# Graph attention layer: the last 20 nodes' four head pairs in one step instead of four

## The chip, the core and the metric

The kernel runs on one core of a Trainium2 chip. TensorE multiplies matrices (its array has 128 rows and 128 columns and can be split into parts that hold different weights), VectorE, ScalarE (ACT) and GpSimd (POOL) work on elements, and SyncE (SP) issues most of the DMA transfers. Each engine works through its own instructions in order and waits on semaphores for the others. The metric is the device time of one execution in microseconds; the time of the kernel before is the median of three runs.

## The reference

Four graph layers follow one another on 2708 nodes with 512 features, each with a residual and a layer norm. The change touches layer 0 alone, an attention over the neighbours with 8 heads of 64 features:

```python
adj = jnp.maximum(adjacency_matrix, jnp.eye(n))
keys    = jnp.einsum('nj,hjk->hnk', node_matrix, Wks)
queries = jnp.einsum('nj,hjk->hnk', node_matrix, Wqs)
values  = jnp.einsum('nj,hjk->hnk', node_matrix, Wvs)
atts = jnp.einsum('hqk,hmk->hqm', queries, keys) / key_dim ** 0.5
atts = atts - 1e+16 * (1.0 - adj)[None, :, :]
atts = jax.nn.softmax(atts, axis=-1)
return jnp.einsum('hqm,hmk,hko->qo', atts, values, Wo)
...
x = _layernorm(x + _L0_gnn_ref(x, adj, ...), axis=-1)
```

Every node's query meets the keys of all 2708 nodes, in every head; the mask lets only neighbours count.

## The kernel before, in words

**Projections.** Keys, values and queries of all nodes are computed first. Keys stay in the on-chip memory as `KT` (features on partitions, two heads of 64 on the two halves of 128), values as `V`, queries go out to memory (`qtd`).

**Items.** The nodes are cut into 22 chunks of 128 rows; the last has 2708 - 21*128 = 20. An item (line 447) is one chunk `c` and one of four head pairs `p`, so there are 88. The class `Pair` (line 276) holds an item's steps. The 2708 keys are taken in three batches of 1024, 1024 and 660, each in two parts of at most 512[...].

- `scores` (line 293): for each part, two products on TensorE, one for each head `j` on its half of the array's rows (line 308), then two reductions on VectorE (line 316) that add the mask, write the scores and keep the row maximum. In the last chunk only 20 partitions are used; there POOL first clears the scores' tile.
- `maxima` (331), then `weights` (338): ACT takes the exponential and the row sums, which go to `smt`.
- `blocks` (353) and `deal` (363): for the first two batches, VectorE transposes blocks of 32x32, and SP moves them by DMA so that keys lie on partitions. `turn` (369): the third batch is transposed by TensorE (382, 389, 391) and copied by ACT (383, 392, 393).
- `values` (398): the weights times `V`, 22 chunks of keys for two heads, summed up on TensorE (410); ACT copies the sum (420) and POOL stores it (421). There is one such accumulator, so a new item's first sum waits for the old item's copy.

**Order.** The loop at line 452 writes out the order for TensorE, VectorE and ACT by hand. In iteration `i` four items are in flight: `new` (item `i`) has its scores made, `cur` (item `i-1`) its exponentials, transposes and deals, `late` (item `i-2`) the third and first batch's values, `old` (item `i-3`) the second batch's values and its copy. After the last item three iterations follow that have no new scores. SP and POOL are ordered by the scheduler. The next chunk's adjacency rows and queries are loaded (`load_chunk`, 153) and prepared (row sums 167, diagonal 176, mask 184) while a chunk's four items run.

**Heads' sums.** `heads_sums` and `heads_rows` (425, 438) turn the inverse row sums of half of the chunks into rows in memory (`rs_d`), in the middle and after the last item.

**What follows layer 0's loop.** For each chunk (line 588) SP loads the stored sums (591), the residual (592) and the broadcast inverse row sums (596); POOL multiplies (599), TensorE maps with `Wo` (602), VectorE adds the residual and applies the layer norm. Layers 1 to 3 come after that and are the same in both kernels.

Of the kernel before, what the change touches and what calls it, by code (L numbers as in the profile page):

```python
# [8 lines left out]
F32 = mybir.dt.float32  # L9
# [13 lines left out]
def kernel(  # L23
# [103 lines left out]
    for t in smt:  # L127
        nc.vector.memset(t, 1.0)
    rs_d = [
        dram.tile([c1 - c0, 2, NP, P], F32, tag=f"rs_d{c0}", name=f"rs_d{c0}") for c0, c1 in ((0, HALF0), (HALF0, NC))  # L130
    ]
    otd = [dram.tile([P, NP, rows(c)[1]], F32, tag=f"otd{c}", name=f"otd{c}") for c in range(NC)]
    with ExitStack() as l0:
# [19 lines left out]
        def load_chunk(c, k):  # L153

            r0, q = rows(c)
            if k == 0:
                a = adjp.tile([P, N], F32, tag="adj", name=f"adj{c}")
                qt = io.tile([P, NP, P], F32, tag="qt", name=f"qt{c}")
                loaded[c] = (a, qt)
            a, qt = loaded[c]  # L160
            if k < NW:
                n0, w = batch(k)
                nc.sync.dma_start(a[:q, n0 : n0 + w], adj[r0 : r0 + q, n0 : n0 + w])
            else:
                nc.sync.dma_start(qt[:, :, :q], qtd[c])

# [9 lines left out]
        def loops(c, k):  # L176

            r0, q = rows(c)
            a = loaded[c][0]
            n0, w = batch(k)  # L180
            if n0 <= r0 < n0 + w:
                nc.vector.tensor_tensor(a[:q, r0 : r0 + q], a[:q, r0 : r0 + q], ident[:q, :q], ALU.max)

        def mask(c, k):

            q = rows(c)[1]
            n0, w = batch(k)
            a = loaded[c][0][:q, n0 : n0 + w]
            nc.scalar.activation(a, a, AF.Identity, scale=1e16, bias=far[:q])
# [86 lines left out]
        class Pair:  # L276


            def __init__(self, c, p):
                self.c, self.p = c, p  # L280
                self.q = rows(c)[1]
                self.groups = (self.q + 31) // 32
# [9 lines left out]

            def scores(self, k, part):

                c, p, q = self.c, self.p, self.q
                a, qt = loaded[c]
                n0, w = batch(k)
                if part == 0:
                    s = sp.tile([P, 2, SW], F32, tag="s", name=f"s{c}_{p}_{k}")
                    if q < P:  # L300
                        nc.gpsimd.memset(s[: 32 * self.groups, :, :w], 0.0)
                    self.s.append(s)
# [4 lines left out]
                for j in range(2):  # L307
                    nc.tensor.matmul(  # L308
                        pss[j][:q, :hw],
                        qt[j * KD : (j + 1) * KD, p, :q],  # L310
                        KT[j * KD : (j + 1) * KD, p, n0 + h0 : n0 + h0 + hw],
                        start=True,
                        stop=True,
                    )
                for j in range(2):
                    nc.vector.tensor_tensor_reduce(  # L316
                        out=s[:q, j, h0 : h0 + hw],
                        in0=pss[j][:q, :hw],
                        in1=a[:q, n0 + h0 : n0 + h0 + hw],
# [4 lines left out]
                        accum_out=self.mx[j][:q, 2 * k + part : 2 * k + part + 1],  # L324
                    )

            def maxima(self):
                c, p, q = self.c, self.p, self.q
                self.nm = [small.tile([P, 1], F32, tag=f"nm{j}", name=f"nm{c}_{p}_{j}") for j in range(2)]
                for j in range(2):  # L330
                    nc.vector.tensor_reduce(self.nm[j][:q], self.mx[j][:q], AX.X, ALU.max, negate=True)  # L331

            def weights(self, k):

                c, p, q, nm = self.c, self.p, self.q, self.nm
                w = batch(k)[1]
                for j in range(2):
                    nc.scalar.activation(  # L338
                        self.s[k][:q, j, :w],
                        self.s[k][:q, j, :w],  # L340
                        AF.Exp,
                        bias=nm[j][:q],
                        accum_out=smt[c // HALF0][:q, c % HALF0, 2 * p + j, k : k + 1],
                    )

            def blocks(self, k, j):

                if k not in self.D:
                    n = ends[k + 1] - ends[k]
                    self.D[k] = dp.tile([P, KD4, 2, n, 32], F32, tag="d", name=f"d{self.c}_{self.p}_{k}")  # L350
                b = 32 * self.groups
                n = ends[k + 1] - ends[k]
                nc.vector.transpose(  # L353
                    self.D[k][:b, :, j].rearrange("p i m x -> p m i x"),
                    self.s[k][:b, j, : n * P].rearrange("p (m i x) -> p m i x", i=KD4, x=32),
                )

            def deal(self, k):
# [3 lines left out]
                for g in range(self.groups):  # L362
# [6 lines left out]
            def turn(self):  # L369

                c, p, q = self.c, self.p, self.q
# [3 lines left out]
                def part(j, m):  # L375
                    return self.s[2][:q, j, (m - ND) * P : (m - ND) * P + P]

                for j in range(2):
                    pt = ps_t.tile([P, last - ND, P], F32, tag="t", name=f"pst{c}_{p}_{j}")
                    sb = ptp.tile([P, last - ND, P], F32, tag="pt", name=f"pt{c}_{p}_{j}", bufs=2)  # L380
                    for m in range(ND, last):
                        nc.tensor.transpose(pt[:, m - ND, :q], part(j, m), ident[:q, :q])  # L382
                    nc.scalar.copy(sb[:, :, :q], pt[:, :, :q])  # L383
                    for m in range(ND, last):
                        self.pts[m, j] = sb[:, m - ND, :q]
                pt = ps_t.tile([P, 4, P], F32, tag="t", name=f"pst{c}_{p}_2")
                sb = ptp.tile([P, 2, P], F32, tag="pt2", name=f"pt{c}_{p}_2")
                for j in range(2):
                    nc.tensor.transpose(pt[:, j, :q], part(j, last), ident[:q, :q])
                for j in range(2):  # L390
                    nc.tensor.transpose(pt[:mr, 2 + j, :q], self.s[2][:q, j, o : o + mr], ident[:q, :q])
                nc.scalar.copy(sb[:, :, :q], pt[:, :2, :q])
                nc.scalar.copy(lastT[:mr, :, :q], pt[:mr, 2:, :q])
                for j in range(2):
                    self.pts[last, j] = sb[:, j, :q]
                    self.pts[NC - 1, j] = lastT[:, j, :q]

            def values(self, m0, m1):
                c, p, q = self.c, self.p, self.q
                if self.av is None:  # L400
                    self.av = ps_a.tile([P, P], F32, tag="av", name=f"av{c}_{p}")
                for m in range(m0, m1):
                    for j in range(2):
                        h = 2 * p + j
                        if m < ND:
                            f = max(f for f in self.E if f <= m)
                            x = self.E[f][:, :, j, m - f, :] if q == P else self.E[f][:, 0, j, m - f, :q]
                        else:
                            x = self.pts[m, j]
                        nc.tensor.matmul(  # L410
                            self.av[j * KD : (j + 1) * KD, :q],
                            V[:, m, h * KD : (h + 1) * KD],
                            x,
                            start=(self.done == 0),
                            stop=(self.done == NC - 1),
                        )
                    self.done += 1
                if self.done == NC:
                    ot = io.tile([P, P], F32, tag="ot", name=f"ot{c}_{p}")
                    nc.scalar.copy(ot[:, :q], self.av[:, :q])  # L420
                    nc.gpsimd.dma_start(otd[c][:, p, :], ot[:, :q])  # L421
# [3 lines left out]
        def heads_sums(i):  # L425

            c0, c1 = (0, HALF0) if i == 0 else (HALF0, NC)
            rs = small.tile([P, NC - HALF0, 2 * NP], F32, tag="rs", name=f"rs{i}", bufs=1)[:, : c1 - c0, :]
            nc.vector.tensor_reduce(
                rs.rearrange("p c h -> p (c h)"), smt[i].rearrange("p c h k -> p (c h) k"), AX.X, ALU.add  # L430
# [16 lines left out]
        items = [(c, p) for c in range(NC) for p in range(NP)]  # L447
        old = late = cur = None
        with tc.manual_schedule(
            engines={mybir.EngineType.PE, mybir.EngineType.DVE, mybir.EngineType.Activation}  # L450
        ):
            for i in range(len(items) + 3):
                new = None
                prep = i < len(items) and items[i][0] + 1 < NC and items[i][1] > 0
                if cur is not None:
                    cur.weights(0)
                if i < len(items):
# [3 lines left out]
                    new = Pair(c, p)  # L461
# [31 lines left out]
                if i in (HALF0 * NP + 2, len(items) + 1):  # L493
                    sums = heads_sums(i > HALF0 * NP + 2)
                if cur is not None:
                    cur.turn()
                if i in (HALF0 * NP + 3, len(items) + 1):
                    heads_rows(*sums)
                old, late, cur = late, cur, new
# [28 lines left out]

    LR = rows(NC - 1)[1]
# [704 lines left out]
```

## Time and profile before

The page is of one profiled execution. Busy time is the share of the span in which an engine had an instruction in work; TensorE's ends are modelled, so its busy time says little about how fast it works. Times in the rows are counted from the start of the span.

| | before |
|---|---|
| time, median of 3 runs | 2624.93 us (2623.91 to 2626.01) |
| the profiled execution: its own time / its span | 2626.93 us / 2625.1 us |
| mean granted clock of TensorE | 0.987 of full speed |
| busy: TensorE, VectorE, ACT, POOL | 2558.7, 1907.4, 1231.2, 332.4 us |
| scores' products, line 308 | 2112 instructions, 484.4 us busy |
| scores' reductions, line 316 | 1056 instructions, 594.4 us busy |
| block transposes, line 353 | 352 instructions, 416.4 us busy |
| first store of a weighted sum / last | 267.5 us / 1283.1 us |
| first product of the last chunk's scores | 1219.15 us |
| first product of the stage after the loop | 1287.38 us |

In a row of the instructions in order of time stand the start, the time that it and its like took together, the engine, the line and operation, the tile written and those read, the part of the array used (rows*columns) with the moving data's shape, and how many instructions are merged. In brackets stands the idle time before it and what ended that. A row of a stretch gives each engine's busy time in it with the number of instructions, the clock granted to TensorE (1.00 is full), the share of time in which the DMA engines were busy, and what they moved.

### The profile page before, as it was taken

How to read it: one execution, taken by the hardware profiler on the slowest of the kernel's cores; microseconds unless marked ns; L12 is line 12 of the kernel's file. 1: busy time of each engine (PE TensorE's matmuls, PEld its weight loads, DVE VectorE, ACT ScalarE, POOL GpSimd, SP SyncE). 2: the span in 40 equal slices, each digit the busy share in tenths (PEclk: the TensorE clock that was granted, in tenths of full speed). 3: DMA queues.
4: the chain of work that ended last, by engine and by line, in shares of the span. 5: the costliest groups of instructions: out<-in, count | busy, mean ns of one | idle time of the engine just before them, and what ended most of it. 6: DMA issues, size and time to landing. Idle time of an engine off the chain costs nothing. (4 is left out here: it accounts for less than half of the span.)

```text
span 2625.1 us, 42264 instructions
## 1 busy us (share of the span) xinstructions
PE 2558.7 (97%) x15298; PEld 1476.8 (56%) x15298; DVE 1907.4 (73%) x4661; ACT 1231.2 (47%) x2464; POOL 332.4 (13%) x336
## 2 busy tenths in 40 slices
PE   8999999999999999999899999899999999999997
PEld 3445677666767676666447444444444456444465
DVE  2004999999999999999684678978767775453544
ACT  1113878788787887877311001566655540000000
POOL 1110000000000000002220000234333330000000
PEclk9999999999999999999799999999999999999999
DMA  5012888888888888887572444354434213644533
GB/s 198 32 53 64 216 233 209 235 211 216 228 214 221 220 208 235 213 212 169 153 240 62 130 122 141 107 166 144 118 101 135 61 30 108 181 142 144 175 100 105
DMA packets 220040, 410.46 MB, mean 156 GB/s; under 512 B 27456, under 2 KB 47664, under 8 KB 219832
## 3 DMA queue, kind: packets, MB, share of 16 engines
q1 hardware_dynamic: 213528, 391.03, 55.4%
q0 software_dynamic: 6304, 16.74, 1.8%
q8 instruction: 121, 1.98, 0.3%
q14 instruction: 87, 0.71, 0.1%
HBM read 212.57 MB, written 16.73 MB: 87 GB/s over the span
## 5 line engine op out<-in xcount | busy, mean ns | idle before, releaser
L316 DVE CUSTOM_DVE_ANT_0 s<-pss,adj 128x512 f32<-128x512 f32 (+3 forms) x1056 | 594.4, 617 | 29.8 <-PE pss L308 27.9
L338 ACT ACTIVATE s<-s,nm 128x1024 f32<-128x1024 f32 (+1 forms) x528 | 546.3, 1037 | 22.2 <-DVE nm L331 20.9
L308 PE MATMUL pss<-KT,qt 64*128 64x512 f32 (+3 forms) x2112 | 484.4, 567 | 6.4 <-DVE mx L316 6.2
L353 DVE STREAM_TRANSPOSE d<-s 128x1024 f32<-128x1024 f32 (+1 forms) x352 | 416.4, 1221 | 6.9 <-DMA e<-d 2.6
L656 PE MATMUL acc<-pt,x 128*128 128x512 f32 (+1 forms) x880 | 338.4, 544 | 12.3 <-ACT pt L709 9.7
L410 PEld LDWEIGHTS av<-e,V 128*64 128x64 f32 x5632 | 306.7, 139 | 66.0 <-issue 34.0
L410 PE MATMUL av<-e,V 128*64 128x128 f32 (+1 forms) x5632 | 339.1, 273 | 0.0
L308 PEld LDWEIGHTS pss<-KT,qt 64*128 64x128 f32 (+1 forms) x2112 | 196.0, 182 | 152.7 <-issue 72.9
L656 PEld LDWEIGHTS acc<-pt,x 128*128 128x128 f32 x880 | 160.0, 194 | 190.3 <-issue 165.3
L762 PE MATMUL acc<-at,h 128*128 128x512 f32 (+1 forms) x504 | 196.8, 543 | 0.0
L720 POOL TENSOR_TENSOR cs<-cs,pt 128x512 f32<-128x512 f32 (+2 forms) x110 | 157.5, 1432 | 202.3 <-ACT pt L709 199.9
L421 POOL DMA_DIRECT2D otd<-ot x88 | 47.3, 538 | 950.7 <-ACT ot L420 938.3
L707 DVE TENSOR_TENSOR pt<-pt,at 128x512 f32<-128x512 f32 (+2 forms) x132 | 107.4, 821 | 79.3 <-ACT pt L706 79.2
L1096 ACT ACTIVATE z<-pz,rdeg 128x512 f32<-128x512 f32 (+1 forms) x22 | 15.1, 688 | 311.0 <-PE pz L668 311.0
L93 ACT ACTIVATE ln_t<-lnve 128x1 f32<-128x1 f32 x88 | 17.7, 201 | 305.0 <-DVE lnve L107 304.9
L383 ACT COPY pt<-pst 128x512 f32<-128x512 f32 (+1 forms) x176 | 92.1, 572 | 127.3 <-PE pst L382 127.1
L762 PEld LDWEIGHTS acc<-at,h 128*128 128x128 f32 x504 | 90.2, 190 | 101.4 <-issue 99.0
L410 PEld LDWEIGHTS av<-pt,V 128*64 128x64 f32 x1760 | 93.6, 138 | 69.6 <-ACT adj L172 46.2
L709 ACT ACTIVATE pt<-pt 128x512 f32<-128x512 f32 (+2 forms) x132 | 76.2, 579 | 107.8 <-DVE pt L708 107.6
L410 PE MATMUL av<-pt,V 128*64 128x128 f32 (+1 forms) x1760 | 114.3, 276 | 3.6 <-ACT ot L420 3.6
L773 DVE SCALAR_TENSOR_TENSOR cs<-at,rdeg,cs 128x512 f32<-128x512 f32 (+2 forms) x126 | 86.2, 684 | 41.4 <-DMA at<-in_adjT_dram 40.5
L85 DVE COPY KT<-psk 128x512 f32<-128x512 f32 (+1 forms) x12 | 7.5, 628 | 138.5 <-PE psk L209 138.5
(282 smaller groups left out, 3559.5 us busy)
## 6 DMA issues: line engine op xcount, KB each, us to landing
e<-d SPq DMA_DIRECT2D x680, 256.0 KB
at<-in_adjT_dram SPq DMA_DIRECT2D x210, 256.0 KB
a<-in_adj_dram SPq DMA_DIRECT2D x38, 677.0 KB
adj<-in_adj_dram SPq DMA_DIRECT2D x42, 512.0 KB
at_a<-in_adjT_dram SPq DMA_DIRECT2D x40, 256.0 KB
at_c<-in_adjT_dram SPq DMA_DIRECT2D x40, 256.0 KB
at_f<-in_adjT_dram SPq DMA_DIRECT2D x40, 256.0 KB
adj<-in_adj_dram SPq DMA_DIRECT2D x21, 330.0 KB
```

Of the source, the lines that this page charges most:

```text
L308: nc.tensor.matmul(pss[j][:q, :hw], qt[j * KD : (j + 1) * KD, p, :q], KT[j * KD : (j + 1) * KD, p, n0 + h0 : n0 + h0 + hw], start=True, st ...
L316: nc.vector.tensor_tensor_reduce(out=s[:q, j, h0 : h0 + hw], in0=pss[j][:q, :hw], in1=a[:q, n0 + h0 : n0 + h0 + hw], scale=1.0, scalar=LOW ...
L338: nc.scalar.activation(self.s[k][:q, j, :w], self.s[k][:q, j, :w], AF.Exp, bias=nm[j][:q], accum_out=smt[c // HALF0][:q, c % HALF0, 2 * p ...
L353: nc.vector.transpose(self.D[k][:b, :, j].rearrange("p i m x -> p m i x"), self.s[k][:b, j, : n * P].rearrange("p (m i x) -> p m i x", i=K ...
L383: nc.scalar.copy(sb[:, :, :q], pt[:, :, :q])
L410: nc.tensor.matmul(self.av[j * KD : (j + 1) * KD, :q], V[:, m, h * KD : (h + 1) * KD], x, start=(self.done == 0), stop=(self.done == NC - 1),)
L656: nc.tensor.matmul(acc[k][:, :w], last[0][g : g + mr, :] if m == NC - 1 else values[:mr, k * P : (k + 1) * P], moving[g : g + mr, :w], sta ...
L707: nc.vector.tensor_tensor(pt[:mr, :w], pt[:mr, :w], at[:mr, :w], ALU.subtract)
L709: nc.scalar.activation(pt[:mr, :w], pt[:mr, :w], AF.Exp)
L720: nc.gpsimd.tensor_tensor(sums[:mr, :w], sums[:mr, :w], pt[:mr, :w], ALU.add)
L762: nc.tensor.matmul(acc[hc][:, :w], lastH[g : g + mr, :] if m == NC - 1 else H[m][:mr, hc * P : (hc + 1) * P], at[g : g + mr, :w], start=(m ...
L773: nc.vector.scalar_tensor_tensor(sums[:mr, :w], at[:mr, :w], rdeg[:mr, m : m + 1], sums[:mr, :w], ALU.mult, ALU.add)
```

## The change

The last chunk has one item instead of four. Its 128 partitions are cut into four groups of 32; group `p` holds the 20 rows for head pair `p`, followed by 12 rows of the chunk before, whose results are not stored.

- **Loads.** The last chunk's adjacency rows are loaded once for each group: the 20 rows and the 12 rows as two transfers, so 8 for each batch and 24 in all, where there were 3; the queries take two transfers where there was one. In SP's queue eight of these loads now stand ahead of each of the deals of the chunk before's first three items.
- **Scores.** A new class `Last` makes, for each part of a batch, eight products in place of two: pair `p` and head `j` work on the part of the array with rows `64*j` to `64*j+63` and columns `32*p` to `32*p+31`. The reductions, exponentials, block transposes, deals and transposes are those of a full chunk, once instead of four times.
- **Values.** The weighted sums stay 20 columns wide and separate for each pair; they use the four accumulators that held scores. The four pairs follow one another inside `values`. Four copies and one store of 512 pieces end it.
- **Row sums.** Those of the last chunk get a tile and rows of their own (`smz`, `rz_d`, `last_sums`); the sums of chunks 11 to 20 are sent out one iteration after the last item's scores.
- **Gone:** POOL's clearing of the scores' tiles for the last chunk; the instructions' narrower forms.

```diff
         def load_chunk(c, k):
...
-                nc.sync.dma_start(a[:q, n0 : n0 + w], adj[r0 : r0 + q, n0 : n0 + w])
+                if c < LAST:
+                    nc.sync.dma_start(a[:q, n0 : n0 + w], adj[r0 : r0 + q, n0 : n0 + w])
+                    return
+
+                for g in range(NP):
+                    for d, r, n in ((0, r0, LR), (LR, N - 32, 32 - LR)):
+                        nc.sync.dma_start(
+                            a[32 * g + d : 32 * g + d + n, n0 : n0 + w], adj[r : r + n, n0 : n0 + w]
+                        )
             else:
                 nc.sync.dma_start(qt[:, :, :q], qtd[c])
+                if c == LAST:
+                    nc.sync.dma_start(qt[:, :, q:32], qtd[c - 1][:, :, P - (32 - q) :])
...
+                for g in range(0, P, 32) if c == LAST else (0,):
+                    d = a[g : g + q, r0 : r0 + q]
+                    nc.vector.tensor_tensor(d, d, ident[g : g + q, g : g + q], ALU.max)
...
-                    if q < P:
-                        nc.gpsimd.memset(s[: 32 * self.groups, :, :w], 0.0)
...
+        class Last(Pair):
+            def products(self, pss, n0, w):
+                qt = loaded[self.c][1]
+                for p in range(NP):
+                    for j in range(2):
+                        h = slice(j * KD, (j + 1) * KD)
+                        nc.tensor.matmul(
+                            pss[j][32 * p : 32 * p + 32, :w],
+                            qt[h, p, :32],
+                            KT[h, p, n0 : n0 + w],
+                            start=True,
+                            stop=True,
+                            tile_position=(j * KD, 32 * p),
+                        )
...
+            def values(self, m0, m1):
+                if self.done == 0:
+                    self.avs = [ps_s.tile([P, BLK], F32, tag=f"s{p % 2}", name=f"avz{p}") for p in range(NP)]
+                done = self.done
+                for p in range(NP):
+                    self.done, self.av = done, self.avs[p]
+                    for m in range(m0, m1):
+                        self.add(m, p, slice(0, LR), [self.weight(m, p, j) for j in range(2)])
+                        self.done += 1
+                if self.done == NC:
+                    self.finish()
+
+            def finish(self):
+                ot = io.tile([P, NP, 32], F32, tag="ot", name="otz")
+                for p in range(NP):
+                    nc.scalar.copy(ot[:, p, :LR], self.avs[p][:, :LR])
+                nc.gpsimd.dma_start(otd[self.c], ot[:, :, :LR])
...
-        items = [(c, p) for c in range(NC) for p in range(NP)]
+        items = [(c, p) for c in range(LAST) for p in range(NP)] + [(LAST, 0)]
...
-                if i in (HALF0 * NP + 2, len(items) + 1):
-                    sums = heads_sums(i > HALF0 * NP + 2)
+                if i in (HALF0 * NP + 2, len(items)):
+                    sums = heads_sums(i == len(items))
...
+                if i == len(items) + 1:
+                    last_sums()
```

## The prediction

> **What bounds the kernel now.** I read the page's forty slices first, then the busy times of single stretches around the end of layer 0, then the instructions of those stretches in order of time. The stretches are the iterations of the item loop, cut where the row maxima of an item are done.
>
> ```profile
> core 0: us, PE busy (x) PEld busy (x) DVE busy (x) ACT busy (x) POOL busy (x), PEclk, DMA share, GB/s
> 1183.40:1195.20 11.80, 11.80 (x128) 8.25 (x125) 11.43 (x33) 10.27 (x22) 0.54 (x1) 1.00 0.80 191
> ...
> 1231.00:1242.20 11.20, 10.92 (x126) 6.57 (x124) 10.88 (x29) 7.83 (x20) 4.73 (x5) 1.00 0.63 147
> 1242.20:1253.70 11.50, 10.28 (x124) 5.42 (x125) 11.40 (x31) 7.40 (x20) 5.31 (x5) 1.00 0.28 53
> 1253.70:1265.80 12.10, 12.10 (x126) 5.68 (x126) 11.06 (x28) 6.73 (x15) 4.93 (x4) 0.72 0.25 46
> 1265.80:1274.90 9.10, 5.60 (x102) 5.32 (x100) 7.39 (x17) 7.00 (x18) 0.54 (x1) 0.64 0.34 61
> 1274.90:1282.60 7.70, 7.33 (x124) 6.80 (x121) 0.37 (x3) 0.85 (x5) 1.07 (x2) 0.50 0.95 260
> ```
>
> In a full iteration (first row) VectorE is busy 11.43 of 11.80 us and TensorE all of it: both are the bound. The items of the last 20 rows (rows two to four) take as long, because VectorE's instructions are as wide as ever and only use fewer partitions. Then come two stretches without new scores; in the last one TensorE is alone, its clock granted at 0.50.
>
> ```profile
> 1221.48 1.97 PE L410 MATMUL av<-e,V 128*64 128x128 f32 x32
> 1223.38 1.90 PE L308 MATMUL pss<-KT,qt 64*20 64x512 f32 x8
> ...
> 1253.70 3.57 PE L308 MATMUL pss<-KT,qt 64*20 64x512 f32 x8 [1.18 <-DVE mx L316]
> ...
> 1262.76 1.09 PE L410 MATMUL av<-e,V 128*64 128x20 f32 x32
> ...
> 1278.42 1.88 PE L410 MATMUL av<-e,V 128*64 128x20 f32 x32
> ...
> 1287.38 42.86 PE L602 MATMUL po<-wo_sb,otl 128*128 128x512 f32 x93 [4.87 <-DMA rb<-rs_d]
> 1329.65 15.81 PE L602 MATMUL po<-wo_sb,otl 128*128 128x512 f32 x36
> ```
>
> Each product in the code is two instructions here. A 512-column one that fills the array costs 15.81/36 = 0.44 us. Eight on half-arrays of 64 rows cost 1.90 us, 0.24 each, so the two halves run beside each other. Likewise 128 columns would cost 0.44/4 = 0.11, and the weighted sums, on halves of 64 columns with different moving data, cost 1.97/32 = 0.06. With 20 moving columns they still cost 1.09/32 = 0.034 at full clock and 1.88/32 = 0.059 at half clock; less the 0.27 us tail of the last one, 0.027 and 0.053.
>
> **Removed.** Three of the four iterations with new scores of the last chunk. In the profile the row maxima of its first item end at 1231.95 us and those of its fourth at 1267.72: 35.8 us apart, with VectorE busy throughout. After the change the one item's maxima are the fourth's; what follows 1231.95 is then compared with what follows 1267.72. SP issues as many deals (8 against 8), and the memsets of POOL (1.8 us each, beside other work) go: nothing.
>
> **Before those maxima.** VectorE's twelve reductions of the item are the old ones (20x512 took 672 ns, 128x512 617), as are ACT's masks: nothing. The diagonal on four groups adds three operations of 0.12 us to a full VectorE: +0.4. The loads are 24+2 transfers in place of 3+1, and in SP's queue they stand eight at a time ahead of the deals of the three items before, whose readers wait behind them. The 20-row loads took 0.34 to 1.04 us to issue, mostly 0.57; eight of 0.4 to 0.6 are 3.2 to 4.8 us per iteration. SP waited 2.5+0.6 = 3.1 us for VectorE in the iteration from 1183.4, so it slips by at most 1.7 each time, 5 us in all; a dealt tile is read 7 us or more after it lands, and its source overwritten 5 us later. I take nothing; without that cover it is up to 3.
>
> The open cost is the scores: 48 products (96 instructions) on 64x32 parts, where one item had 12 (24). The trace has no such part. From below: all eight parts run at once and a 512-column step stays 0.95 us, as each part streams what a half did; 0 added (less is excluded, since every part still streams 512 columns). From above: all in turn, eight times two times 0.43. [...] But the row of 1221.48 shows two column halves on the same 128 rows, with different weights, at 0.06 where one by one is 0.11. I follow the row: near the lower end, +1 for the issue of four times as many instructions (16 of 0.034 = 0.5 us per step, under the 0.95 it streams). So the maxima come at 1231.95 + 0.4 + 1 = 1233.3; call it T.
>
> **After T.** ACT's chain is the one of before: from 1267.72 to the end of its last exponential at 1273.97, 6.3 us, exponentials of 128 partitions taking what those of 20 did. An old item's copy stands between the first two and the rest (0.27, was 0.15), and the sums of the next-to-last item wait for it; they (56 of 0.054 = 3.0) end before the exponentials do. Then the transposes, now 128 wide (1216.54 to 1218.1, 1.5 us, half of it ahead of the last exponential): T+7.5. The sums' second part of the item before: 32 of 0.054, T+9.3. Then the new part: all four pairs' weighted sums, 4 x 88 = 352 instructions of 20 columns. Before there were as many, but half of them lay beside VectorE's work and 176 came after 1267.72; now all come after T. At full clock 352 x 0.027 = 9.4 us; at half, 18.8. Their data is there: blocks of VectorE end at T+6.4, the deals land by T+13, and these are read last.
>
> Which clock? [...] from 1274.9 to 1282.6 TensorE was busy 7.33 of 7.70 us with just these instructions and stayed at 0.50. But it gets there from 128-column work at 1.00, and a stretch at 1247.8 to 1251.2 with 1.8 us of 20-column sums kept 1.00. I take a drop after about 3 to 4 us: 130 at 0.027 and 222 at 0.053 = 15.3. TensorE ends layer 0 at T+9.3+15.3 = 1257.9, where it ended at 1282.5: 24.6 gained. Ends: 1252 (all at full) and 1264.5 (half already from T+6 on).
>
> **The hand-over.** Before, the next stage's first product waits 4.87 us after that, for a broadcast that was queued with 1 MB of weights. Now those loads are issued from about T+11 and are landed at the end; what remains is a copy (0.2), the POOL store of 512 pieces (0.8 by the stores of queries with 512 pieces, 0.54 now), the product on POOL that stands behind it (1.26) and gaps of 0.3: 2.6. Gain 2.3. That stage is bound by TensorE (42.5 of 42.6 us), so an earlier start is kept, and later layers only shift. The separate row sums of the last rows (under 1 us on an idle VectorE, a broadcast half a stage later): nothing.
>
> Sum: 24.6 + 2.3 = 27 (26.9). The profiled execution (span 2625.1, own time 2626.93) becomes about 2600; against the median of 2624.93, which is 2.0 lower, the prediction is 2598.
>
> **Rivals.**
> A, the above: 2598, with its clock cases 2592 to 2605. Chance 0.74.
> B, only pairs overlap: [...] four moving streams are too many for one row half. TensorE, which has no room in that iteration, takes 13.6 more, less the 1 counted: 2611 (with half the overlap 2602; with a low clock too, 2617). For it: no row shows four column parts. Against it: the 1.8-fold overlap of two. Chance 0.18.
> C, slower than before: the parts run one after another[...]. Then a 512 step is 6.9 us and the item's scores 36 instead of 4.6, +32; and such thin work lost the clock before (scores of 64x20 took 3.57 instead of 1.90 us from 1253.7), so up to twice that: 2629 to 2665, say 2640. It decides from the point where the scores cost over 27 us more, at about 6 us per 512-column step, that is where eight parts overlap less than 1.15-fold. Against it stands every overlapping row above. Chance 0.04.
> D, the time isn't kept: late deals from the crowded SP queue hold TensorE and VectorE in the three items before by some 5 us each and the clock drops there, 2612 to 2622. Against it: the slack of 5 to 7 us. Chance 0.04.
>
> **Numbers.** Runs of this kernel differ by some 0.1%, so about 0.2% (5.2 us) is what a measurement can tell from no change. Faster by more, under 2619.7: A, nearly all of B, half of D: 0.93. Within: the slow edges of B and D: 0.04. Slower: most of C, 0.03. The range reaches from A with full clock and a cheap hand-over, 2590, to B at 2613, which leaves out B's slow edge, C and half of D.
>
> **What would show it.** The scores' instructions of the last item: eight of 64x512 on 32 columns within 0.5 us of issue and steps near 1 us (A), 3.4 us (B), 6.9 us (C). The maxima of the last item at about 1233 us. VectorE's reductions waiting for TensorE there means B or C. The granted clock while the 352 sums run, and their 9.4 to 18.8 us. The first product of the next stage some 2.6 us after the last sum. I am wrong if the last maxima come after 1240 us, if the sums wait for deals, or if the next stage's first product waits for its loads as long as before.

## The result, and the profile after

The changed kernel takes 2604.99 us (median of 6 runs, 2600.6 to 2611.59) against 2625.47 us for the kernel before beside it (6 runs): ratio 0.9921 [0.9906, 0.9936], 20.5 us faster. The prediction was 2598, with 2590 to 2613. The profiled execution has an own time of 2611.59 us and a span of 2609.8, the longest of the six; the span of before's is 2625.1. The span is 15.3 us shorter.

The busy times of stretches of the changed kernel, cut where the maxima of an item are done and where TensorE's work changes (columns as in the first view of the prediction):

```profile
core 0: us, PE busy (x) PEld busy (x) DVE busy (x) ACT busy (x) POOL busy (x), PEclk, DMA share, GB/s
1213.80:1230.10 16.30, 13.93 (x138) 8.61 (x136) 13.06 (x45) 10.06 (x22) 0.54 (x1) 1.00 0.88 200
1230.10:1241.50 11.40, 11.40 (x197) 7.73 (x190) 11.40 (x33) 7.86 (x17) 0.54 (x1) 1.00 0.70 159
1241.50:1251.20 9.70, 6.36 (x95) 5.44 (x91) 6.01 (x12) 8.34 (x19) 0.54 (x1) 1.00 0.88 205
...
1254.20:1261.30 7.10, 7.08 (x220) 6.99 (x217) 0.00 (x0) 0.27 (x1) 0.56 (x1) 0.91 0.92 244
1261.30:1269.60 8.30, 6.14 (x137) 5.76 (x136) 0.00 (x0) 0.78 (x4) 0.52 (x1) 0.77 1.03 274
```

The second row is the new item's iteration: 11.40 us, with four times as many scores' instructions in it and VectorE busy throughout. The first of before's narrow items took 11.3, so the added instructions cost next to nothing. The first row is the item before it, and there the loss shows: 16.30 us, of which TensorE stands idle for 2.4 and VectorE for 3.2. The last two rows are the 352 sums of 20 columns: the clock is full for about two thirds of their time, and in the last row TensorE is idle for 2.2 of 8.3 us.

The instructions behind these rows, TensorE of the changed kernel in order of time:

```profile
1228.65 2.62 PE L448 MATMUL pss<-KT,qt 64*32 64x512 f32 x32 [1.63 <-DVE mx L332]
...
1233.10 1.95 PE L448 MATMUL pss<-KT,qt 64*32 64x512 f32 x32
...
1251.18 0.28 PE L503 MATMUL prs<-ident,riTrue 128*80 128x128 f32 x1 [1.90 <-DVE rz L511]
...
1257.58 3.69 PE L417 MATMUL avz<-e,V 128*64 128x20 f32 x120
1263.11 0.41 PE L417 MATMUL avz<-e,V 128*64 128x20 f32 x8 [1.83 <-issue]
...
1263.65 4.87 PE L417 MATMUL avz<-e,V 128*64 128x20 f32 x119
1268.87 0.72 PE L417 MATMUL avz<-e,V 128*64 128x20 f32 x9 [0.34 <-issue]
1272.17 3.78 PE L677 MATMUL po<-wo_sb,otl 128*128 128x512 f32 x4 [2.58 <-POOL otl L674]
```

The row of 1233.10 is two 512-column steps on all eight parts of 64x32: 32 instructions in 1.95 us, where the eight of before took 1.90. One by one at the prediction's 0.43 each (15.81 us for 36 full-array products in before, less the last one's tail) they would take 13.8, so the overlap is 7-fold. The other rows are taken up below: a wait for the row sums (1.90), sums with a hole in which nothing that the profile shows is waited for (1.83), and a hand-over of 2.58 us in place of 4.87.

Put together, in us. The maxima are counted from the end of an item's last maximum reduction, as in the prediction. A runs from the maxima of the 80th item to those of the last, B from there to TensorE's end of layer 0, C to the next stage's first product, D to the end of the span.

| profiled execution | 80th maxima | intervals between maxima in A | A | B | C | D | span |
|---|---|---|---|---|---|---|---|
| before | 1172.1 | 11.5 11.8 11.7 13.5, then 11.3 11.7 11.5 12.6 | 95.6 | 14.8 | 4.9 | 1337.8 | 2625.1 |
| after | 1175.3 | 11.5 13.6 13.6 16.3, then 11.4 | 66.4 | 27.9 | 2.6 | 1337.7 | 2609.8 |

Up to the 80th maxima both do the same work, and the 3.2 us by which they differ there are scatter between executions: with the same work up to that point, before_loads (below) has them at 1175.8, and the other versions but one at 1173.4 to 1183.3. In A 35.8 us of iterations go (11.7, 11.5 and 12.6), and 6.5 come back in the four before (55.0 for 48.5). The tail B is 13.1 longer, as all sums now stand behind the last item; the hand-over is 2.3 shorter. 3.2 - 29.2 + 13.1 - 2.3 - 0.1 = -15.3.

### The profile page after: what moved, and what is told of

It is laid out like the page before. It is cut to its first block, busy times and chain, and to the rows that moved or that the text cites. A ratio compares the mean times of both kernels' runs of the same rounds, so it can differ in the third digit from the quotient of the medians.

```text
span 2609.8 us, 42027 instructions
## 1 busy us (share of the span) xinstructions
PE 2540.3 (97%) x15263; PEld 1472.2 (56%) x15263; DVE 1874.5 (72%) x4576; ACT 1212.1 (46%) x2417; POOL 312.0 (12%) x322
## 4 chain that ended last, share of the span: by engine, by line
PE 77%; issue 9%; DVE 6%; DMA 4%; SPq 2%; ACT 1%; POOL 0%; POOLq 0%; DVEq 0%; ACTq 0%
PE pss L310 15%; PE av L417 14%; PE acc L731 13%; PE acc L837 7%; PE m L1141 6%; PE pf L743 3%; PE psv L250 3%; PE psk L223 3%; PE pst L390 3%; PE psq L223 3%; DMA e<-d 2%; PE po L677 2%; PE ph L823 1%; DVE d L361 1%; SPq L371 1%
## 5 line engine op out<-in xcount | busy, mean ns | idle before, releaser
L332 DVE CUSTOM_DVE_ANT_0 s<-pss,adj 128x512 f32<-128x512 f32 (+1 forms) x1020 | 574.2, 618 | 27.6 <-PE pss L310 26.5
L354 ACT ACTIVATE s<-s,nm 128x1024 f32<-128x1024 f32 (+1 forms) x510 | 527.7, 1037 | 22.9 <-DVE nm L347 22.0
L310 PE MATMUL pss<-KT,qt 64*128 64x512 f32 (+1 forms) x2016 | 463.8, 565 | 7.7 <-DVE mx L332 7.4
L361 DVE STREAM_TRANSPOSE d<-s 128x1024 f32<-128x1024 f32 x340 | 402.4, 1222 | 18.1 <-DMA e<-d 9.0
L731 PE MATMUL acc<-pt,x 128*128 128x512 f32 (+1 forms) x880 | 341.0, 547 | 12.6 <-ACT pt L784 9.7
L417 PEld LDWEIGHTS av<-e,V 128*64 128x64 f32 x5376 | 295.6, 137 | 62.6 <-issue 32.9
L417 PE MATMUL av<-e,V 128*64 128x128 f32 x5376 | 327.4, 275 | 0.0
L310 PEld LDWEIGHTS pss<-KT,qt 64*128 64x128 f32 x2016 | 194.2, 186 | 145.3 <-issue 69.3
L391 ACT COPY pt<-pst 128x512 f32<-128x512 f32 x170 | 91.5, 589 | 120.9 <-PE pst L390 120.5
L417 PE MATMUL av<-pt,V 128*64 128x128 f32 x1680 | 110.3, 278 | 1.4 <-ACT ot L437 1.4
```

The costliest lines, as they stand in the source:

```text
L310: nc.tensor.matmul(pss[j][:, :w], qt[h, self.p, :], KT[h, self.p, n0 : n0 + w], start=True, stop=True)
L332: nc.vector.tensor_tensor_reduce(out=s[:, j, h0 : h0 + hw], in0=pss[j][:, :hw], in1=a[:, n0 + h0 : n0 + h0 + hw], scale=1.0, scalar=LOW, o ...
L354: nc.scalar.activation(s, s, AF.Exp, bias=self.nm[j], accum_out=self.sums(j, k))
L361: nc.vector.transpose(self.D[k][:, :, j].rearrange("p i m x -> p m i x"), self.s[k][:, j, : n * P].rearrange("p (m i x) -> p m i x", i=KD4 ...
L391: nc.scalar.copy(sb, pt)
L417: nc.tensor.matmul(self.av[j * KD : (j + 1) * KD, out], V[:, m, h * KD : (h + 1) * KD], weights[j], start=(self.done == 0), stop=(self.don ...
```

## Experiments

**Theory.** The scores overlap almost fully. What is missing is lost ahead of the last item, because the loads of few rows stand in SP's queue ahead of the deals, so that VectorE's transposes and TensorE's sums wait for late deals. **Rivals:** the loads' bytes or their effect on the memory take the time wherever they are issued; or the low clock in the tail takes it.

VectorE's waits of the kernel before, then of the one after, from 1172 to 1242 us (columns: what waits and for what, us in total, times, longest):

```profile
DVE s L316 <- PE pss L308: 1.4, 4, 0.4
DVE dg_t L96 <- ACT dg_y L94: 0.5, 1, 0.5
```

```profile
DVE d L361 <- issue: 2.5, 1, 2.5
DVE d L361 <- ACT ot L437: 2.4, 2, 1.6
DVE d L361 <- DMA e<-d: 1.4, 2, 0.8
DVE dg_t L96 <- ACT dg_y L94: 0.5, 1, 0.5
```

Three new lines, all on the block transposes (line 361), 6.3 us together: the size of the loss in A. The third names deals; the first two name nothing that a transpose needs (line 437 copies a weighted sum). The landings settle it. A tile of transposed blocks goes out in four deals and may be overwritten only when all four have landed. The five pairs of transposes that waited, at 1190.52, 1196.14, 1204.40, 1209.78 and 1218.98, begin 0.12 to 0.18 us after the last of these landings (1190.34, 1196.02, 1204.22, 1209.66, 1218.80). In the kernel before, from 1174 to 1216, the landing is always 0.5 to 2.1 us ahead of the transpose. The clock is at 1.00 all through A, so the second rival is out for this loss. SP's instructions of the changed kernel in that time:

```profile
1191.24 5.09 SPq L172 DMA_DIRECT2D adj<-in_adj_dram  x8
1196.45 9.26 SPq L371 DMA_DIRECT2D e<-d  x8
1205.75 4.81 SPq L172 DMA_DIRECT2D adj<-in_adj_dram  x8
1210.67 8.81 SPq L371 DMA_DIRECT2D e<-d  x8
```

Eight loads and eight deals follow each other without a gap: 14.5 us from 1191.24 to 1205.75 and 13.7 from there to the end of the next eight deals, about the length of an iteration (13.6). From 1186.6 to 1230.1 SP waited 3.1 us in all; before it had waited 15.8.

**The loads alone** (before_loads): the kernel before with the changed kernel's 24+2 loads, and nothing else. The added rows are loaded into partitions that it does not read.

```diff
-                nc.sync.dma_start(a[:q, n0 : n0 + w], adj[r0 : r0 + q, n0 : n0 + w])
+                if c < NC - 1:
+                    nc.sync.dma_start(a[:q, n0 : n0 + w], adj[r0 : r0 + q, n0 : n0 + w])
+                    return
+                for g in range(NP):
+                    for d, r, n in ((0, r0, q), (q, N - 32, 32 - q)):
+                        nc.sync.dma_start(
+                            a[32 * g + d : 32 * g + d + n, n0 : n0 + w], adj[r : r + n, n0 : n0 + w]
+                        )
...
+                if c == NC - 1:
+                    nc.sync.dma_start(qt[:, :, q:32], qtd[c - 1][:, :, P - (32 - q) :])
```

> The kernel before, with only the last chunk's loads as the change makes them: 24+2 transfers in place of 3+1, the partitions above the 20th being loaded and not used. If the loads in SP's queue hold back the deals of the three items after them (the theory), the intervals between the row maxima of these items grow from 11.7 to about 13.6 us, VectorE waits there, and the kernel is some 6 to 8 us slower than before, at 2631 to 2633. If they are harmless (the loss of the changed kernel comes from the new item), the intervals stay at 11.7 and the time at 2625.

Measured: 2631.93 against 2627.53 us (22 and 27 runs), ratio 1.0016 [1.0010, 1.0023], so +4.4 us. The four intervals are 11.5, 13.0, 13.3 and 15.3 (53.1 for 48.5, +4.6), the later ones 11.3, 11.7, 11.5 and 12.3 as before. That is less than the 6 to 8 us expected, but the loads cost by themselves most of what the change lost in A, without any of its other parts.

**The same loads from POOL's queue** (pool_loads): in the changed kernel, `nc.sync.dma_start` becomes `nc.gpsimd.dma_start` for the 24 adjacency loads. Bytes, shapes and number stay.

> The changed kernel with its 24 adjacency loads issued from POOL's queue instead of SP's; same bytes, same pieces, same place in the order. If SP's issue time is what delays the deals (the theory), the intervals of the three items return to about 11.7 us and the time falls by 6 to 8 us against the changed kernel, to about 2597. If the bytes or the small pieces themselves crowd the DMA engines (the rival), the deals land as late as before and the time stays near 2605.

Measured in the profile: intervals 12.8, 11.6, 11.6 and 14.1 (50.1 where after had 55.0 and before 48.5). SP's instructions of this kernel:

```profile
1183.49 44.80 SPq L371 DMA_DIRECT2D e<-d  x30
```

Only deals stand there, and SP waited 17.6 us from 1186.6 to 1230.1, where after it was 3.1. The same bytes now cost 1.6 of the 6.5 us, so most of the loss comes from what stands ahead of the deals in their queue. The four intervals add up to 53.1 to 55.0 us in all six executions with these 24 loads on SP, and to 50.1 and 50.7 in the two with POOL's. What is left has another cause: a tile's deals that were all issued by 1179.2 landed only at 1185.55, 6.4 us later (4.6 for the same tile of before, 1174.3 to 1178.9), while POOL's loads were under way. Whether their bytes or their pieces do that is open; and POOL issues the last eight at 1194 to 1198, where SP did at 1206 to 1211, so their time has moved too. The expected 6 to 8 us did not come in the measured time: 2606.76 us (2599.21 to 2614.73), ratio 0.9922 [0.9902, 0.9942], beside 0.9926 for the change run again. The queue's part is thus shown by the profile and by before_loads, not by this time; a gain of 5 us is within the scatter of these versions, much of which is explained at the end.

**Eight long loads from SP** (long_loads): if the number of issues is the cost, 8 transfers of whole rows instead of 24 help.

```diff
-                for g in range(NP):
-                    for d, r, n in ((0, r0, LR), (LR, N - 32, 32 - LR)):
-                        nc.sync.dma_start(
-                            a[32 * g + d : 32 * g + d + n, n0 : n0 + w], adj[r : r + n, n0 : n0 + w]
-                        )
+                if k == 0:
+                    for g in range(NP):
+                        for d, r, n in ((0, r0, LR), (LR, N - 32, 32 - LR)):
+                            nc.sync.dma_start(a[32 * g + d : 32 * g + d + n, :], adj[r : r + n, :])
```

> The changed kernel with the last chunk's adjacency rows loaded by 8 transfers over all 2708 columns instead of 24 over a batch each; same bytes, all ahead of the first of the three items' deals. If SP's issue time per transfer is the cost (the theory), SP is held up once by 3 to 5 us, and the three intervals after it sum up to some 5 us less than the 43.4 us of the changed kernel. If the bytes are the cost (the rival), the sum stays.

Measured: 2608.6 us (2600.92 to 2611.94), 0.9922 [0.9907, 0.9936]; intervals 12.5, 16.1, 13.6 and 14.4, 56.6 together. This sum is too high to compare: in this execution the clock stood at half from 1203.0 to 1209.9, within these items. The later kernel with the same loads (fixed) kept the full clock here and has 53.4, which is still no better than 24 loads. So the number of issues is not the cause by itself. SP's deals waited for the landing of the loads ahead of them, 3.4 us in 6 waits (5.5 in 8 in fixed), while in after none of SP's 3.1 us of waits is for a load's landing, and its eight loads take some 5 us to issue. Landing and issue were not tried apart.

**The change again** (after_again), with no edit, to see what it scatters.

> The changed kernel once more, beside the others on one chip, as their measure. 2601 to 2607 us; in the profile the intervals of the last chunk's three preceding items near 13.6 us again if that loss is steady, near 11.7 if it was of that one execution.

Measured: 2607.35 us (2604.14 to 2616.18), 0.9926 [0.9909, 0.9943]. Intervals 11.5, 12.5, 13.8 and 15.7 (53.5), with SP again waiting for only 2.6 us from 1186.6 to 1230.1; B is 30.0.

**32 columns in the sums** (wide_sums, wide_again): the last item's sums stream 32 columns instead of 20. The 12 more are computed and not stored.

```diff
-                    return self.pts[m, j][:, 32 * p : 32 * p + LR]
+                    return self.pts[m, j][:, 32 * p : 32 * p + 32]
...
-                        self.add(m, p, slice(0, LR), [self.weight(m, p, j) for j in range(2)])
+                        self.add(m, p, slice(0, 32), [self.weight(m, p, j) for j in range(2)])
```

> The changed kernel with the last item's weighted sums 32 columns wide instead of 20 (the 12 columns more are not stored). [...] the 352 sums cost 0.027 us each at full clock as with 20 columns, the clock stays at 1.00, and they take 10 us instead of 15: 5 us faster than the changed kernel. If the clock falls whatever the width (the rival), they take 15 us again and the time stays; if the pace follows the columns, they take longer.

Measured: 2598.93 us (2596.71 to 2606.81), 0.9895 [0.9878, 0.9912], the fastest version so far, and its clock stayed at 1.00 until the sums were done (1265.6). I took that for proof that columns hold the clock, and ran it once more.

> wide_sums once more, beside fixed_pool on the same chip: what it scatters. Both theories: ratio 0.988 to 0.992; fixed_pool 3 to 6 us below it if the loads' place in SP's queue costs, the same if not. The clock should again stay at 1.00 through the last item's sums if the columns that are streamed decide it; a half-clock stretch inside those sums would speak against that.

Measured: 2600.52 us (2598.98 to 2606.35), 0.9905 [0.9891, 0.9919]. But the clock did fall, at 1253.9 and again at 1267.5. This kernel's busy times, cut where the clock's record changes, and then those of the version below that moves the row sums (20 columns):

```profile
1247.10:1250.50 3.40, 3.33 (x50) 2.92 (x47) 1.45 (x2) 3.33 (x8) 0.00 (x0) 1.00 0.82 178
1250.50:1253.90 3.40, 1.31 (x15) 0.88 (x15) 2.67 (x6) 1.50 (x5) 0.00 (x0) 1.00 0.91 208
1253.90:1257.30 3.40, 3.40 (x44) 3.40 (x40) 0.00 (x0) 0.27 (x1) 0.54 (x1) 0.50 0.86 227
1257.30:1260.70 3.40, 3.40 (x123) 3.40 (x121) 0.00 (x0) 0.00 (x0) 0.56 (x1) 1.00 0.87 234
```

```profile
1249.40:1252.80 3.40, 3.40 (x124) 3.40 (x122) 0.00 (x0) 0.00 (x0) 0.00 (x0) 1.00 0.82 216
1252.80:1256.20 3.40, 1.90 (x63) 1.80 (x60) 0.00 (x0) 0.00 (x0) 0.00 (x0) 1.00 0.94 277
1256.20:1259.60 3.40, 3.40 (x58) 2.92 (x54) 0.00 (x0) 0.26 (x1) 0.54 (x1) 0.50 0.99 313
1259.60:1263.00 3.40, 3.40 (x70) 3.40 (x68) 0.00 (x0) 0.00 (x0) 0.00 (x0) 0.50 1.00 288
```

In both, a stretch of 3.4 us in which TensorE is idle for 1.5 to 2.1 us is followed by one at half clock; so a narrow product is not needed for a fall. In the second, 124 instructions of 20 columns run in a stretch at full clock. In the first, the clock is full again (1257.3) after a stretch that is mostly 128-column sums; in the second it is still at half (1259.6) after a stretch of almost nothing but 20-column sums, though TensorE counts as busy for all of it. So my reading of wide_sums fell. The 32 columns are some 6 us faster in both runs than the two runs of the change, though the intervals of the pairs touch or overlap. Some 2 us of that have a cause beside the width: POOL's queue, which the scheduler orders, has its first product ahead of the last item's store in the four kernels with 32 columns and the last chunk at the end (wide_again: product at 1268.81, store at 1272.26) and behind it in those with 20 (after: store at 1270.10, product at 1270.79), so that C is 1.0 in wide_sums and 0.3 in wide_again instead of 2.6. The rest is not settled.

**The row sums later** (rows_later): the row sums of chunks 11 to 20 are turned and sent one iteration later, so that in TensorE's queue they stand behind most of the last sums instead of ahead of them.

```diff
-                if i in (HALF0 * NP + 3, len(items)):
+                if i in (HALF0 * NP + 3, len(items) + 1):
```

> The changed kernel with TensorE's transposition of the heads' row sums moved one iteration on, behind the last item's first 224 sums. In the changed kernel TensorE waited 1.9 us for VectorE's reciprocal ahead of them. If that wait is on the path (the theory), TensorE starts the last sums some 2 us earlier after the last maxima and the time falls by 2 us, to about 0.992 of before less 0.001; if the sums then wait for their own data instead (the rival), for the same time, nothing is gained.

Measured: 2605.08 us (2602.35 to 2606.5), 0.9910 [0.9896, 0.9924]. B is 26.4 instead of 27.9 and 30.0: the new part's first sums start 9.3 us after the maxima (12.5 in after), though the clock then fell once more. The measured time cannot tell the 2 us expected. The wait of 1.90 us was the row sums' (the releaser that the profile names, line 511, ended beside their reciprocal, at 1251.05). Those were late because VectorE's last blocks were, in the changed kernel:

```profile
1243.56 2.37 DVE L361 STREAM_TRANSPOSE d<-s 128x1024 f32<-128x1024 f32 x2 [1.85 <-DMA e<-d]
1247.69 2.37 DVE L361 STREAM_TRANSPOSE d<-s 128x1024 f32<-128x1024 f32 x2 [1.76 <-DMA e<-d]
```

They wait for full-width deals with no reductions between that would hide it; before, the last item's narrow blocks had waited only for ACT's exponentials (1.26 us). The fixed_pool kernel below has the same waits (1.90 and 1.77), so they do not come from the crowded queue.

**Together** (fixed: long loads, 32 columns, later row sums; fixed_pool: POOL's loads, 32 columns, later row sums).

> The changed kernel with 8 long loads, sums 32 columns wide and the row sums' transposition one iteration later. If the three losses are separate and add up, some 12 to 15 us under the changed kernel: 0.987 of the time before. If the loads or the wait are hidden by what is late next, only the 8 us of the wide sums stay: 0.9895.

Measured: 2603.01 us (2601.37 to 2605.24), 0.9904 [0.9890, 0.9918]. This is neither the 0.987 of three losses that add up nor better than the 32 columns alone (0.9895, 0.9905). B is 22.5, the shortest with the last chunk at the end, but A keeps the loss of the long loads (11.5, 16.3, 11.3, 14.3), and C grows to 4.4 (its lines are numbered one lower):

```profile
1261.98 0.57 PE L416 MATMUL avz<-e,V 128*64 128x32 f32 x9 [1.95 <-issue]
1266.91 2.93 PE L676 MATMUL po<-wo_sb,otl 128*128 128x512 f32 x3 [4.36 <-POOL otl L673]
```

Here TensorE ends earlier, but the next stage does not start as much earlier: POOL's product waited until 1265.59 for the row sums that are now sent later. 1.8 us of the tail's gain goes back there.

> The change with the three edits that each took one cost away: the last chunk's 24 adjacency loads from POOL's queue, 32 columns in the last item's weighted sums, and the last chunks' row sums one iteration later. If what stands ahead of the deals in SP's queue is what costs, the four intervals of the maxima from the 80th item on are near 11.8, 11.7, 11.7 and 13.5 (48 to 51 us together, as in pool_loads), the TensorE tail after the last maxima near 22.6 us as in fixed, and VectorE's blocks of the last item wait under 1 us for deals. Time then 2593 to 2600, ratio 0.988 to 0.990, at or below wide_sums. If the order in the queue were not the cause, the intervals would be 54 to 57 as in all the versions that load from SP, and the time 2600 or more.

Measured: 2600.16 us (2594.53 to 2605.41), 0.9897 [0.9880, 0.9913], against 0.9905 for wide_again on the same chip. In the profile the stretches came as expected, 12.5, 12.5, 11.3 and 14.4 (50.7; wide_again 53.9) and a tail B of 23.0; but the blocks' waits did not go, and the expected 3 to 6 us between the two did not show in the time, as they did not in pool_loads. In these two executions, fixed_pool's 80th maxima come 5.1 us later (1183.3 to 1178.2) for the same work, and C and D take 6.1 more.

**The last chunk's item first** (last_first): its narrow sums then lie beside the next items' scores instead of in the tail. This also takes 32 columns, one accumulator, the later row sums, and loads of the last chunk during the projections.

```diff
-        items = [(c, p) for c in range(LAST) for p in range(NP)] + [(LAST, 0)]
+        items = [(LAST, 0)] + [(c, p) for c in range(LAST) for p in range(NP)]
```

> The one item of the last chunk is done first instead of last: its rows are loaded during the projections, its 352 sums (32 wide, in one accumulator) lie beside the next items' work, and an ordinary item of 128 columns ends the loop. If the serial sums at the end and the crowded SP queue are what is left to gain (the theory), the time falls by some 17 us against the changed kernel, to 0.985 of before: the end of the loop comes some 14 us after the last maxima instead of 28, and the third and fourth iterations are 1 to 2 us longer. If TensorE, full in these early iterations, hands the 352 sums' whole 9.4 us on to VectorE (the rival), about 8 us of it are lost again and it stays near 0.988.

Measured: 2609.06 us (2607.86 to 2613.65), 0.9926 [0.9912, 0.9939], no gain. The tail is 18.9 us, but the first maxima come at 250.4 instead of 240.7, since TensorE waits 7.05 us for queries that have only just been written to memory; the third and fourth iterations take 14.1 and 13.7 (12.4 and 11.3 in after), and the hand-over takes 7.3. What the tail gave was lost at the start.

## Why the prediction was right, and where not

**Removed (35.8): held.** The three iterations are gone, and one of 11.4 us stands where the first of the old last chunk's took 11.3.

**Reductions, masks, diagonal (+0.4), scores (+1, between 0 and 13.6): the lower end held.** The last iteration has no room in which those 1.4 us could hide, and is 0.1 longer; the two terms were taken too high by nearly their whole size. The upper end was my estimate for pairs that follow one another: some three times an item's 4.6 us of scores more, and 8 x 0.43 = 3.4 us for a 512-column step. No row had shown that, and it did not come: the step took 0.98 us (0.95 in before). The row of two column halves was the better guide, and rivals B and C fell.

**Loads ("I take nothing; without that cover it is up to 3"): this step failed.** It cost 6.5 us in this profile (4.6 to 6.5 in the six executions with these loads on SP) and 4.4 us [2.6 to 6.0, from the ratio's interval] by itself in before_loads. Two things were wrong. The slip is not at most 1.7 per iteration: eight loads and eight deals fill SP's 13.6 us, so that SP sets the iteration's length. And the slack was counted to the deal's issue, while its source may be overwritten only when it has landed: in the profile of before a tile's last deal is issued by 1192.9, lands at 1196.1, and the transpose that overwrites its source starts at 1198.2; for the item's other tile these are 1197.6, 1202.3 and 1202.9. Where I saw 5 us there were 2.1, and 0.6. Rival D was the right mechanism at under half of its size (6.5 for three times 5), and without its low clock: the rows of A stay at 1.00.

**T = 1233.3: came at 1241.7,** 8.4 later: 6.5 for the loads, 3.2 for the scatter up to the 80th maxima and 0.1 for the last iteration, less the 1.4 for scores and diagonal that are not seen. So one of the prediction's own signs of being wrong, maxima after 1240, came true; without the scatter they would have come at 1238.5.

**After T (24.6 from T to TensorE's end): 27.9.** The old sums end at T+12.5 instead of T+9.3. Of these 3.2 us, 1.90 are the wait for the row sums of chunks 11 to 20, for which the prediction has no term. It puts only the last rows' own at "nothing", because VectorE is idle then. But VectorE was idle because it waited for deals (1.85 and 1.76 us), its row sums stand behind the blocks that were so delayed, and TensorE's queue stands behind the transpose of the row sums. Most of the rest is the old sums' 3.07 us, mostly at half clock, after that wait. The 1.7 counted for them were 32 at the 0.054 of 20 columns at half clock, but they are a full chunk's, 128 columns wide. The 352 sums then took 15.4 us, for 15.3 predicted, but not by the predicted course: they ran at full clock for about two thirds of the way, and lost time to two holes (1.83 and 0.34 us) and to the half clock at the end. The figure held by chance.

**The clock.** From two places in the trace of before (20-column sums that stay at 0.50 from 1274.9 to 1282.6, and 1.8 us of them in a stretch that kept 1.00) I took a drop "after about 3 to 4 us" of such sums; that length was my estimate, and no run shows it. The clock was at 1.00 for 10 us of such sums in after (1255.5 to 1265.8), and nearly every drop follows a stretch of 3.4 us with 0.8 us or more of idle time of TensorE. The reverse does not hold. I cut all twelve executions, from 235 us to TensorE's end, into stretches on the grid of the last section and took those that began at full clock: with more than 2.0 us idle, all 32 were followed by half clock; with 0.8 to 2.0 us, 41 of 200; with less, 3 of some 7900. (TensorE's ends are modelled, so these idle times are rough.) So in these runs idle time above 2 us always cost the clock, and below it something else decides as well. In after_again the drop at 1263.7 came after a stretch with 118 sums and no idle time, so idle time does not account for every drop. Once at half, a stretch of almost nothing but these sums was followed by half clock again: 59 instructions from 1265.8 in after, 68 from 1267.1 in after_again, 58 from 1256.2 in rows_later.

**The hand-over (2.6): 2.58.** Its end is POOL's product behind the store, as predicted, though that order is the scheduler's and changed with the 32 columns. That an earlier start is kept holds too: D is 1337.7 after 1337.8.

The sum by its own terms: 24.6 + 2.3 = 27 (26.9) predicted; from this 8.4 (T) and 3.3 (tail) are to be taken off and 0.1 (D) put back: 15.3 measured in the profiles. By the medians it is 20.5, and 2604.99 us lies inside the range, at the slow end of rival A's own cases (2592 to 2605). Part of that is luck: the range's slow side was drawn for rival B, which did not happen, and what filled it were the loads and the wait for the row sums, which the prediction had put at nothing or left out.

## What to carry to other kernels

A queue's slack has to be counted to the time when a transfer lands, and for who overwrites its source, not only for who reads its target (here 0.6 to 2.1 us, where I had counted 5); and a queue that waits for some 4 us of an 11.7-us iteration (15.8 of 43.5 here) is full after eight loads that take 5. Small transfers are better kept out of the queue whose transfers the inner loop waits for: here that took 5 of the 6.5 us off in the profile. If work is packed into fewer and wider steps, look at the tail: what lay beside other work before may now all stand at the end, where a wait can also cost the clock (in after the 1.90 us for the row sums, then 3.4 us at half).

## What the runs showed of the hardware

**The clock's drops lie whole multiples of 3.413 us apart, and they are much of the scatter.** In every execution all drops begin on such a grid (after: 248.6, 1252.1, 1265.8, 1671.9 and so on, with the same remainder). In the clock's record of before and of after, each time at half clock that ends within the span also lasts 3.413 us (6 of 9 in before, 5 of 8 in after) or a multiple of it (6.827, 10.240, 23.893). One wait of TensorE was followed by half clock in one execution and by full clock in another, and lay differently on the grid: a wait of 3.64 us in the later layers (line 641). In the changed kernel nearly all of it lies in one stretch, and the clock falls after it:

```profile
1668.00:1671.90 3.90, 0.30 (x2) 0.30 (x3) 3.90 (x7) 2.49 (x4) 2.40 (x3) 1.00 0.24 69
1671.90:1675.30 3.40, 3.40 (x6) 1.35 (x5) 3.40 (x5) 1.40 (x3) 0.76 (x1) 0.51 0.13 17
```

In wide_sums the same wait, from 1659.5 to 1663.1, is shared by two stretches of the grid, and the clock stays full in the one after them:

```profile
1658.09:1661.50 3.41, 1.41 (x4) 0.34 (x2) 3.41 (x6) 1.28 (x3) 1.99 (x2) 1.00 0.50 145
1661.50:1664.91 3.41, 1.77 (x6) 1.05 (x7) 3.41 (x4) 3.00 (x5) 2.62 (x2) 1.00 0.01 2
1664.91:1668.33 3.42, 3.42 (x9) 0.84 (x8) 3.05 (x7) 1.55 (x4) 0.91 (x1) 1.00 0.28 77
```

D is the same code in all versions, but took 1327.3 to 1338.1 us. Less half of the time at half clock in it (up to TensorE's last instruction), the twelve executions lie between 1320.1 and 1324.1. Some of them:

| execution | D | of it at half clock | D less half of that |
|---|---|---|---|
| before | 1337.8 | 28.7 | 1323.4 |
| after | 1337.7 | 27.7 | 1323.8 |
| after_again | 1338.1 | 31.8 | 1322.2 |
| pool_loads | 1332.8 | 18.0 | 1323.9 |
| wide_sums | 1330.5 | 19.6 | 1320.7 |
| wide_again | 1327.8 | 9.1 | 1323.3 |
| fixed_pool | 1331.8 | 17.0 | 1323.4 |

So differences of some 5 us between versions cannot be told from such luck by a few runs, and are read from the profile's stretches instead. This also bears on the two runs with 32 columns, whose D is among the shortest. Not all scatter is the clock's: the 80th maxima, which come after the same work in eleven executions, lie between 1172.1 and 1183.3, and there the clock accounts for under 2 us.

**Holes in dense runs of small products.** The last sums' idle times put down to "issue" (1.83 us in after, 1.95 in fixed, 2.9 in wide_sums, up to 4.0 in long_loads) mostly begin within about 1.4 us of a 16 KB packet of the instruction queue's (at 1260.60 in after, the hole at 1261.28; at 1265.53 in fixed_pool, the hole at 1265.51), while the DMA engines are 91 to 106% busy with the next stage's loads. The traces show this coincidence and not what the holes wait for, and no run tested a cause.
